# An LSTM recurrence on one core: gate banks by halves, four tanh, and output sums by accumulating transfers

## The chip, the core and the metric

The kernel runs on one core of a Trainium2 chip. A core has TensorE (PE, with its weight loads shown as PEld), VectorE (DVE), ScalarE (ACT), GpSimd (POOL) and SyncE (SP), which only issues transfers; ACT and POOL issue transfers too. The engines run beside each other and wait for each other by semaphores. The metric is the device time of one execution, in microseconds (us), the median of several runs.

## What is computed

Two layers over x of shape (32, 512, 256), fp32: 32 batch rows, 512 places, 256 features. Each layer adds a graph attention block and then a feed-forward block to x. The first three of these four blocks make the first two thirds of the time and are not touched by the change. The fourth block is an LSTM over the 512 places, followed by running sums:

```python
x_proj = jnp.einsum('btd,gd->btg', x, W_ih) + b_ih + b_hh
def step(carry, xp):
    h, c = carry
    gates = xp + h @ W_hh.T
    i, f, g, o = jnp.split(gates, 4, axis=-1)
    c = jax.nn.sigmoid(f) * c + jax.nn.sigmoid(i) * jnp.tanh(g)
    h = jax.nn.sigmoid(o) * jnp.tanh(c)
    return ((h, c), h)
...
logits = jnp.einsum('bth,lh->btl', lstm_out, W_lin) + b_lin
g = jax.lax.stop_gradient(jnp.argmax(logits, axis=-1).astype(lstm_out.dtype))[..., None]
w = g * lstm_out
inc = jnp.cumsum(w, axis=1)
prefix = inc - w
suffix = inc[:, -1:, :] - inc
return 2.0 * lstm_out + prefix * fw_att + suffix * bw_att
```

The x that goes in is a layer norm of the layer's x, and the result is added to x. There are two logits, so that `g` is 0 or 1.

## The kernel before

The first stage (`layers_per_batch`) goes through the 32 batch rows and leaves x in device memory as X3 (places, batch, features). In it, POOL prepares the LSTM's weights piece by piece (`recurrence_weights`, lines 1180 to 1287): it scales the gates, lays them out in the order g, f, i, o (`order`, `half`, `ordered`) and writes them to `wr`.

The second stage is `recurrence` (line 1290 on). The 256 features are four quarters q of 64, and each quarter is two halves of H = 32. All tiles of a step have 128 partitions: 4 quarters x 32 batch rows. Column tiles of PE (32 output partitions each) make the four quarters.

Gates stand in two banks of PSUM (`PARTS`, line 1406): bank 0 has g, f, i of the first halves (96 columns), bank 1 has g, f, i of the second halves, o of both halves, and two columns that carry the logits (162 columns). `part` (line 1408) multiplies one operand into the banks, in an order of pairs (k, n): k is the half of the contraction, n the bank, each with four matmuls, one for each quarter. All matmuls are fp32.

A step t of the loop at line 1444 does this:

1. PE adds the part of `h` to the banks of step t, in the order (0,0), (0,1), (1,0), (1,1) (line 1465); `h[0]` and `h[1]` are the transposed halves of the last step. Then it starts the banks of step t + 1 with the part of x (`x_part`, line 1418).
2. ACT takes tanh of bank 0 (line 1472, 96 columns) and of bank 1 (line 1473, 160 columns). The sigmoids are tanh too, by scaled weights.
3. VectorE makes, for each half, `ab` (line 1478) and the new c in `z2` (line 1481).
4. ACT takes tanh of c for each half (line 1483), and copies one column (line 1485).
5. VectorE makes `hh` (line 1491) and its transpose `h` (line 1495) for each half. These release the next step's matmuls.
6. VectorE makes `g` (line 1502) from the logits in bank 1 and `hh` of the step before, does one filler from the list `extra` (line 1506), and adds to the running sum `pp` (line 1508). At a chunk's first step it also copies `pp` (line 1510).

A chunk is 16 steps (CH), and in each chunk 16 fillers are done, one in each step. Four are statistics of the next chunk's x (`stats`, lines 1335 to 1339; the last one has POOL make `ve` and `rs`, lines 132 and 134), two are norms of two tiles each (`both`, line 1457, with `norm` at line 1341), and ten are the results of the chunk before (`results`, line 1360): in two halves of 8 places, x3 = x3 + hh + pp * fw - pp' * bw, five operations on 512 columns each. The last one is followed by four transfers of x3 to the tile R (line 1399), which holds all outputs. SP loads x (line 1331) and x3 (line 1364). PE turns the normed x in steps 5, 6, 10 and 11 (`turn`, line 1347).

The order of PE, VectorE and ACT is the order of the program's text (line 1425). The order of SP and POOL is made by a scheduler. A buffer that is read by a transfer or another engine is not written before that is done.

After the loop (lines 1511 to 1531), `tot` is the total of the sum times bw (the weights fw and bw are halved at line 1253). 16 transfers spread it over all partitions into `tots`; the last chunk's results follow; and then, in 17 pieces of up to 8 places, VectorE adds `tots` to R and SP and ACT send R to the output.

Of the kernel before, what the change touches and what calls it, by code (L numbers as in the profile page):

```python
# [9 lines left out]
F32 = mybir.dt.float32  # L10
# [9 lines left out]
P = 128  # L20
# [1159 lines left out]
def recurrence_weights(nc, pool, a, wr, now):  # L1180
# [18 lines left out]
    def ordered(raw, n, quarters, s):  # L1199

        t = tile_(P, 2 * W, "rwt")
        tq = t.rearrange("p (q w) -> p q w", q=2)[:n, :quarters]
        rq = raw.rearrange("p (q w) -> p q w", q=quarters)[:n]
        nc.gpsimd.memset(tq[:, :, 4 * J :], 0.0)
        for to, g in enumerate(order):
            src = rq[:, :, g * J : (g + 1) * J]
            if to < 3:
                for e in range(2):
                    nc.gpsimd.tensor_scalar(
                        tq[:, :, (3 * e + to) * 32 : (3 * e + to + 1) * 32], src[:, :, e * 32 : (e + 1) * 32],  # L1210
                        half[g] * s, None, ALU.mult,
                    )
            else:
                nc.gpsimd.tensor_scalar(tq[:, :, 3 * J : 4 * J], src, half[g] * s, None, ALU.mult)
        return t, tq
# [37 lines left out]
    nc.gpsimd.tensor_scalar(t[:, : 2 * J], t[:, : 2 * J], 0.5, None, ALU.mult)  # L1253
# [36 lines left out]
def recurrence(ctx, tc, c, a, X3, wr, out):  # L1290
# [27 lines left out]
    R = wp.tile([P, TQ, D], F32, name="R")  # L1318

# [40 lines left out]
    def results(t0, hh, pp):  # L1360

        x3 = ch.tile([P, CH, J], F32, tag="x3", name=f"x3_{t0}")
        for q in range(Q):
            nc.sync.dma_start(
                out=x3[q * GB : (q + 1) * GB],
                in_=X3[t0 : t0 + CH, :, q * J : (q + 1) * J].rearrange("t b j -> b t j"),
            )
        todo = []
        n = CH // 2
        for s in (slice(0, n), slice(n, CH)):  # L1370
            r = x3[:, s, :]
            pf = pp[:, s.start : s.stop, :]
            pb = pp[:, s.start + 1 : s.stop + 1, :]
            m = st.tile([P, n, J], F32, tag="m", bufs=1, name=f"m{t0}_{s.start}")
            bc = [P, n, J]

            def one_(r=r, s=s):
                nc.vector.tensor_tensor(r, r, hh[:, s, :], ALU.add)  # L1378

            def two_(m=m, pf=pf):  # L1380
                nc.vector.tensor_tensor(m, pf, fw.unsqueeze(1).to_broadcast(bc), ALU.mult)  # L1381

            def three(r=r, m=m):
                nc.vector.tensor_tensor(r, r, m, ALU.add)  # L1384

            def four(m=m, pb=pb):
                nc.vector.tensor_tensor(m, pb, bw.unsqueeze(1).to_broadcast(bc), ALU.mult)  # L1387

            def five(r=r, m=m):
                nc.vector.tensor_tensor(r, r, m, ALU.subtract)  # L1390

            todo += [one_, two_, three, four, five]
        last_ = todo.pop()

        def gathered():
            last_()
            tq, r0 = t0 // TQ, t0 % TQ
            for q in range(Q):
                nc.sync.dma_start(
                    out=R[tq * GB : (tq + 1) * GB, r0 : r0 + CH, q * J : (q + 1) * J], in_=x3[q * GB : (q + 1) * GB]  # L1400
                )

        return todo + [gathered]


    PARTS = ((0, 3 * H), (3 * H, W))

    def part(pg, w, lhs, order, start, stop):

        for k, n in order:  # L1410
            p, (s, e) = pg[n], PARTS[n]
            for q in range(Q):
# [5 lines left out]
    def x_part(t, xT):  # L1418
# [3 lines left out]
        part(pg, wih, [xT[t % CH // G][:, k, r : r + GB] for k in range(DK)], ((0, 0), (1, 0), (0, 1), (1, 1)), True, t == 0)  # L1422
        return pg

    with tc.manual_schedule(engines={mybir.EngineType.PE, mybir.EngineType.DVE, mybir.EngineType.Activation}):
# [18 lines left out]
        for t in range(T + 1):  # L1444
            s = t % CH
            last = t == T
            if s == 0 and not last:
# [9 lines left out]
                both = [lambda fs=norms[n : n + 2]: [f() for f in fs] for n in range(0, len(norms), 2)]  # L1457
                extra = stats + both + more
                turning = {(5, 6, 10, 11)[n]: f for n, f in enumerate(turns)}
            if last:  # L1460

                pg = [None, psg.tile([P, W - 3 * H], F32, tag="pg1", name="pglast")]
                part(pg, whh, h, ((0, 1), (1, 1)), True, True)
            elif t:
                part(pg, whh, h, ((0, 0), (0, 1), (1, 0), (1, 1)), False, True)
            pgs = pg
            if not last:
# [4 lines left out]
                nc.scalar.activation(z[:, H : 4 * H], pgs[0], AF.Tanh)  # L1472
                nc.scalar.activation(z[:, 5 * H : 10 * H], pgs[1][:, : 5 * H], AF.Tanh)
# [23 lines left out]
            if t:  # L1497
# [5 lines left out]
                    g_, pgs[1][:, 5 * H : 5 * H + 1].to_broadcast([P, J]), level, h_[:, i, :], ALU.is_gt, ALU.mult,  # L1503
# [11 lines left out]
        tots = wp.tile([P, D], F32, name="tots")  # L1515
        for n in range(4 * Q):
            tq, q = n // Q, n % Q
            (nc.sync, nc.scalar, nc.gpsimd)[n % 3].dma_start(
                out=tots[tq * GB : (tq + 1) * GB, q * J : (q + 1) * J], in_=tot[q * GB : (q + 1) * GB]
            )  # L1520
        for f in results(T - CH, hh, pp):
            f()
        t0 = 0
        for step in [2, 6] + [8] * (TQ // 8 - 1):
            r = R[:, t0 : t0 + step, :]
            nc.vector.tensor_tensor(r, r, tots.unsqueeze(1).to_broadcast([P, step, D]), ALU.add)  # L1526
# [4 lines left out]
            t0 += step  # L1531

# [123 lines left out]
```

## Time and profile before

| | us |
|---|---|
| median of 3 runs | 3859.15 (3856.74 to 3864.42) |
| the profiled execution | 3853.91 |
| its span | 3852.2 |
| stage 1, from 0 to about 2540 | PE busy 2356.98, DVE 2062.08, ACT 1794.45, POOL 1448.21 |
| recurrence, 2540 to 3787 | PE busy 1060.81, DVE 1152.43, ACT 608.58, POOL 59.84 |
| tail, 3787 to 3853 | DVE busy 41.94, transfers 265 GB/s |

The granted clock of TensorE was 0.98 in stage 1 and 0.99 in the recurrence. Times in the views are microseconds from the start of the span. A row of the timeline has its start, its length, the engine, the line of the kernel, the operation with what it writes and reads, how often it comes in a row, and in brackets the engine's idle time before it with what ended that. A matmul's end is modelled, so starts are the safer numbers. Matmuls of a row that overlap are merged into one length.

### The profile page before, as it was taken

The page shows a single profiled execution, that of the slowest core. Times are in us where ns is not written, and L with a number is a line of the kernel's source. Part 1 is how long each engine was busy: PE and PEld are TensorE (multiplying, and loading weights), DVE is VectorE, ACT ScalarE, POOL GpSimd, SP SyncE. Part 2 cuts the span into 40 slices and gives each one's busy share as a digit, 9 for nine tenths or more (in the row PEclk, how much of TensorE's full clock was granted, in tenths as well). Part 3 has the DMA queues.
Part 4 walks back from the last instruction along what each step waited for, and adds up shares of the span by engine and source line. Part 5 has one row for each costly group of instructions (what it writes and reads, how often), then busy time and mean ns, then how long its engine had stood idle before and what let it go on. Part 6 is the DMA issues. An engine that isn't in the chain of part 4 may idle for free. (4 is left out here: it accounts for less than half of the span.)

```text
span 3852.2 us, 117182 instructions
## 1 busy us (share of the span) xinstructions
PE 3417.8 (89%) x47370; PEld 2313.5 (60%) x47370; DVE 3256.5 (85%) x10671; ACT 2403.0 (62%) x6434; POOL 1510.6 (39%) x1581
## 2 busy tenths in 40 slices
PE   5999999999999999999999998668888888888882
PEld 3466566556656656655665664446666666666661
DVE  3888888888888888888888886459999999999997
ACT  2777777777777777777777775435454544444441
POOL 3456556555555655655555566710000000000000
PEclk8999999999999999999999998789999999999996
DMA  3322322222223232232223212221222222222226
GB/s 98 89 91 73 101 85 75 94 86 86 83 93 90 72 102 86 72 95 86 86 83 96 87 61 59 82 66 41 44 46 43 46 43 46 43 46 43 46 40 191
DMA packets 271800, 288.76 MB, mean 75 GB/s; under 512 B 151589, under 2 KB 221953, under 8 KB 269073
## 3 DMA queue, kind: packets, MB, share of 16 engines
q1 hardware_dynamic: 265248, 266.96, 25.0%
q10 hardware_dynamic: 3152, 8.76, 0.7%
q8 instruction: 375, 6.14, 0.7%
q0 software_dynamic: 2848, 5.45, 0.5%
q14 instruction: 177, 1.44, 0.1%
HBM read 227.09 MB, written 37.11 MB: 69 GB/s over the span
## 5 line engine op out<-in xcount | busy, mean ns | idle before, releaser
L1413 PE MATMUL pg<-wall,h 128*32 128x96 f32 x16352 | 559.0, 277 | 176.8 <-DVE h L1495 169.4
L1413 PEld LDWEIGHTS pg<-wall,h 128*32 128x32 f32 x16352 | 374.4, 109 | 350.8 <-DVE h L1495 331.9
L1413 PE MATMUL pg<-wall,xTr 128*32 128x96 f32 (+1 forms) x16384 | 549.0, 274 | 0.0
L1413 PEld LDWEIGHTS pg<-wall,xTr 128*32 128x32 f32 x16384 | 447.2, 110 | 5.2 <-issue 0.3
L132 POOL TENSOR_SCALAR ve<-mv 128x4 f32<-128x4 f32 x32 | 6.3, 195 | 1038.5 <-DVE mv L1337 1038.5
L1472 ACT ACTIVATE z<-pg 128x96 f32<-128x96 f32 x512 | 128.7, 251 | 438.9 <-PE pg L1413 438.9
L102 DVE SCALAR_TENSOR_TENSOR w<-rb,colsa,adjT 128x512 f32<-128x512 f32 x512 | 380.4, 778 | 6.0 <-DMA rb<-linea 6.0
L102 DVE SCALAR_TENSOR_TENSOR acc<-px,convw,acc 128x511 f32<-128x511 f32 (+2 forms) x480 | 335.3, 735 | 7.6 <-ACT acc L102 6.4
L1483 ACT ACTIVATE z<-z 128x32 f32<-128x32 f32 x1024 | 234.7, 229 | 168.5 <-DVE z L1481 100.9
L102 ACT ACTIVATE g<-bc,cs 128x128 f32<-128x128 f32 x1024 | 326.0, 399 | 13.1 <-PE py L102 13.1
L102 PE MATMUL px<-mT,win 128*128 128x512 f32 x640 | 307.2, 603 | 0.0
L102 PE MATMUL po<-wc,xh 128*128 128x256 f32 x1024 | 254.3, 392 | 13.5 <-POOL xh L102 8.4
L102 POOL TENSOR_SCALAR ve<-bnmv 128x4 f32<-128x4 f32 x96 | 18.8, 196 | 626.3 <-DVE bnmv L102 607.7
L102 PE MATMUL pav<-w,hb 128*64 128x512 f32 x1024 | 250.1, 608 | 8.0 <-DVE w L102 8.0
L102 PE MATMUL pov<-wb,wv 128*128 128x257 f32 x1024 | 250.5, 392 | 7.0 <-DVE wv L102 5.8
L1495 DVE STREAM_TRANSPOSE h<-hh 128x32 f32<-128x32 f32 x1024 | 216.4, 211 | 34.8
L102 PE MATMUL pz<-mT,win 128*128 128x512 f32 x512 | 245.4, 602 | 0.0
L102 POOL TENSOR_TENSOR rs<-ve,mhalf 128x4 f32<-128x4 f32 (+1 forms) x192 | 237.8, 1239 | 13.3
L1478 DVE SCALAR_TENSOR_TENSOR ab<-z 128x64 f32<-128x64 f32 x1024 | 226.0, 221 | 15.3 <-ACT z L1472 12.0
L102 PEld LDWEIGHTS po<-wc,xh 128*128 128x128 f32 x1024 | 189.5, 193 | 76.6 <-issue 27.0
L1481 DVE SCALAR_TENSOR_TENSOR z<-ab 128x32 f32<-128x32 f32 x1024 | 196.9, 192 | 35.1
L102 POOL TENSOR_SCALAR msk<-adj 128x1024 bf16<-128x1024 int32 x64 | 218.8, 3434 | 13.0 <-DMA adj<-in_adj_dram 7.9
(258 smaller groups left out, 7987.8 us busy)
## 6 DMA issues: line engine op xcount, KB each, us to landing
bc<-line SPq DMA_DIRECT2D x128, 512.0 KB
adj<-in_adj_dram SPq DMA_DIRECT2D x32, 1024.0 KB
rb<-linea SPq DMA_DIRECT2D x64, 512.0 KB
ce<-line SPq DMA_DIRECT2D x64, 384.0 KB
x<-in_x_dram SPq DMA_DIRECT2D x32, 512.0 KB
X<-x SPq DMA_DIRECT2D x32, 512.0 KB
xt<-X SPq DMA_DIRECT2D x128, 128.0 KB
x<-X SPq DMA_DIRECT2D x128, 128.0 KB
```

Of the source, the lines that this page charges most:

```text
L102: return getattr(getattr(self.nc, engine), op)(*map(real, a), **{n: real(v) for n, v in k.items()})
L132: nc.gpsimd.tensor_scalar(ve, var, scale, eps, ALU.mult, ALU.add)
L1413: nc.tensor.matmul(p[q * GB : (q + 1) * GB, :], lhs[k], w[:, k, q, s:e], start=(start and k == 0), stop=(stop and k == DK - 1),)
L1472: nc.scalar.activation(z[:, H : 4 * H], pgs[0], AF.Tanh)
L1478: nc.vector.scalar_tensor_tensor(ab, z[:, c0 + 2 * H : c0 + 4 * H], 1.0, z[:, c0 : c0 + 2 * H], ALU.add, ALU.mult)
L1481: nc.vector.scalar_tensor_tensor(z2[:, c0 : c0 + H], ab[:, :H], 0.5, ab[:, H:], ALU.mult, ALU.add)
L1483: nc.scalar.activation(z[:, (10 + n) * H : (11 + n) * H], z2[:, 4 * n * H : (4 * n + 1) * H], AF.Tanh, scale=0.5)
L1495: nc.vector.transpose(h[n], half)
```

## The change

- The gates are laid out as g, f, i, o of the first halves, then g, f, i, o of the second halves and the logits' columns. So bank 0 has 128 columns and bank 1 has 130.
- ACT has four tanh in place of two: of 96 and of 32 columns in bank 0, then of 96 and of 32 in bank 1.
- The matmuls of `h` come in the order (0,0) for all quarters, (0,1) for quarters 0 and 1, (1,0) for all, (0,1) for quarters 2 and 3, (1,1) for all.
- The results are sums by transfers of POOL that accumulate into x3: `hh` as it is, pp * fw, and pp' * bw with the sign of bw turned (line 1253 becomes a multiply by 0.5 and one by -0.5). VectorE only makes the products, in eight fillers of 256 columns; norms are one tile to a filler, and PE turns x in steps 6, 7, 10 and 11. A chunk still has 16 fillers.
- After the loop, `tots` is made by four matmuls with `sel`, a tile of ones and zeros that POOL copies from the identity before the loop. The outputs subtract it. The last chunk's results are done between the first outputs.

```diff
         nc.gpsimd.memset(tq[:, :, 4 * J :], 0.0)
         for to, g in enumerate(order):
             src = rq[:, :, g * J : (g + 1) * J]
-            if to < 3:
-                for e in range(2):
-                    nc.gpsimd.tensor_scalar(
-                        tq[:, :, (3 * e + to) * 32 : (3 * e + to + 1) * 32], src[:, :, e * 32 : (e + 1) * 32],
-                        half[g] * s, None, ALU.mult,
-                    )
-            else:
-                nc.gpsimd.tensor_scalar(tq[:, :, 3 * J : 4 * J], src, half[g] * s, None, ALU.mult)
+            for e in range(2):
+                nc.gpsimd.tensor_scalar(
+                    tq[:, :, (4 * e + to) * 32 : (4 * e + to + 1) * 32], src[:, :, e * 32 : (e + 1) * 32],
+                    half[g] * s, None, ALU.mult,
+                )
         return t, tq
     def begun(t, *columns):
...
         for q in range(Q):
             nc.gpsimd.dma_start(out=t[q * GB : (q + 1) * GB, n * J : (n + 1) * J], in_=src[q : q + 1, :].to_broadcast([GB, J]))
         yield
-    nc.gpsimd.tensor_scalar(t[:, : 2 * J], t[:, : 2 * J], 0.5, None, ALU.mult)
+    for n, scale in enumerate((0.5, -0.5)):
+        nc.gpsimd.tensor_scalar(t[:, n * J : (n + 1) * J], t[:, n * J : (n + 1) * J], scale, None, ALU.mult)
     yield
     nc.gpsimd.dma_start(out=wr[:, n0 : n0 + 2 * J], in_=t[:, : 2 * J])
     yield
...
     TQ = T // 4
     R = wp.tile([P, TQ, D], F32, name="R")
+    sel = wp.tile([P, Q, P], F32, name="sel")
+    for q in range(Q):
+        nc.gpsimd.tensor_copy(
+            sel[:, q, :].rearrange("p (t b) -> p t b", b=GB),
+            c.ident[:, q * GB : (q + 1) * GB].unsqueeze(1).to_broadcast([P, 4, GB]),
+        )
     NX = CH // 4
...
                 out=x3[q * GB : (q + 1) * GB],
                 in_=X3[t0 : t0 + CH, :, q * J : (q + 1) * J].rearrange("t b j -> b t j"),
             )
+        nc.gpsimd.dma_start(out=x3, in_=hh, accum_op=ALU.add)
         todo = []
-        n = CH // 2
-        for s in (slice(0, n), slice(n, CH)):
-            r = x3[:, s, :]
-            pf = pp[:, s.start : s.stop, :]
-            pb = pp[:, s.start + 1 : s.stop + 1, :]
-            m = st.tile([P, n, J], F32, tag="m", bufs=1, name=f"m{t0}_{s.start}")
-            bc = [P, n, J]
-
-            def one_(r=r, s=s):
-                nc.vector.tensor_tensor(r, r, hh[:, s, :], ALU.add)
-
-            def two_(m=m, pf=pf):
-                nc.vector.tensor_tensor(m, pf, fw.unsqueeze(1).to_broadcast(bc), ALU.mult)
-
-            def three(r=r, m=m):
-                nc.vector.tensor_tensor(r, r, m, ALU.add)
-
-            def four(m=m, pb=pb):
-                nc.vector.tensor_tensor(m, pb, bw.unsqueeze(1).to_broadcast(bc), ALU.mult)
-
-            def five(r=r, m=m):
-                nc.vector.tensor_tensor(r, r, m, ALU.subtract)
-
-            todo += [one_, two_, three, four, five]
+        for n, w in enumerate((fw, bw)):
+            m = ch.tile([P, CH, J], F32, tag=f"m{n}", bufs=1, name=f"m{n}_{t0}")
+            for s in range(0, CH, 4):
+
+                def product(n=n, w=w, m=m, s=s):
+                    nc.vector.tensor_tensor(
+                        m[:, s : s + 4, :], pp[:, s + n : s + n + 4, :], w.unsqueeze(1).to_broadcast([P, 4, J]), ALU.mult
+                    )
+                    if s + 4 == CH:
+                        nc.gpsimd.dma_start(out=x3, in_=m, accum_op=ALU.add)
+
+                todo.append(product)
         last_ = todo.pop()
         def gathered():
...
         return todo + [gathered]
-    PARTS = ((0, 3 * H), (3 * H, W))
+    PARTS = ((0, 4 * H), (4 * H, W))
+    ALL = tuple(range(Q))
+    WHOLE = tuple((k, n, ALL) for n in range(2) for k in range(DK))
+    LATER = ((0, 0, ALL), (0, 1, ALL[:2]), (1, 0, ALL), (0, 1, ALL[2:]), (1, 1, ALL))
     def part(pg, w, lhs, order, start, stop):
-        for k, n in order:
+        for k, n, qs in order:
             p, (s, e) = pg[n], PARTS[n]
-            for q in range(Q):
+            for q in qs:
                 nc.tensor.matmul(
                     p[q * GB : (q + 1) * GB, :], lhs[k], w[:, k, q, s:e],
                     start=(start and k == 0), stop=(stop and k == DK - 1),
...
         pg = [psg.tile([P, e - s], F32, tag=f"pg{n}", name=f"pg{n}_{t}") for n, (s, e) in enumerate(PARTS)]
         r = (t % G) * GB
-        part(pg, wih, [xT[t % CH // G][:, k, r : r + GB] for k in range(DK)], ((0, 0), (1, 0), (0, 1), (1, 1)), True, t == 0)
+        part(pg, wih, [xT[t % CH // G][:, k, r : r + GB] for k in range(DK)], WHOLE, True, t == 0)
         return pg
     with tc.manual_schedule(engines={mybir.EngineType.PE, mybir.EngineType.DVE, mybir.EngineType.Activation}):
...
                 xT, nxt = nxt, [None] * 2
                 stats, norms, turns = normalised(t0 + CH, nxt) if t0 + CH < T else ([], [], [])
                 more = results(t0 - CH, hh_was, pp_was) if t else []
-                both = [lambda fs=norms[n : n + 2]: [f() for f in fs] for n in range(0, len(norms), 2)]
-                extra = stats + both + more
-                turning = {(5, 6, 10, 11)[n]: f for n, f in enumerate(turns)}
+                extra = stats + more[:1] + norms + more[1:] if t else stats + norms
+                turning = {(6, 7, 10, 11)[n]: f for n, f in enumerate(turns)}
             if last:
-                pg = [None, psg.tile([P, W - 3 * H], F32, tag="pg1", name="pglast")]
-                part(pg, whh, h, ((0, 1), (1, 1)), True, True)
+                pg = [None, psg.tile([P, W - 4 * H], F32, tag="pg1", name="pglast")]
+                part(pg, whh, h, WHOLE[DK:], True, True)
             elif t:
-                part(pg, whh, h, ((0, 0), (0, 1), (1, 0), (1, 1)), False, True)
+                part(pg, whh, h, LATER, False, True)
             pgs = pg
             if not last:
                 if t + 1 < T:
                     pg = x_part(t + 1, xT if t + 1 < t0 + CH else nxt)
                 turned = [turning.pop(s)()] if s in turning else []
-                nc.scalar.activation(z[:, H : 4 * H], pgs[0], AF.Tanh)
-                nc.scalar.activation(z[:, 5 * H : 10 * H], pgs[1][:, : 5 * H], AF.Tanh)
+                for n in range(2):
+                    nc.scalar.activation(z[:, (4 * n + 1) * H : (4 * n + 4) * H], pgs[n][:, : 3 * H], AF.Tanh)
+                    nc.scalar.activation(z[:, (8 + n) * H : (9 + n) * H], pgs[n][:, 3 * H : 4 * H], AF.Tanh)
                 z2 = st.tile([P, 12 * H + 1], F32, tag="z", name=f"z{t + 1}")
                 for n in range(2):
                     c0 = 4 * n * H
...
                 p_, h_ = (pp_was, hh_was) if s == 0 and not last else (pp, hh)
                 g_ = st.tile([P, J], F32, tag="g", name=f"g{t}")
                 nc.vector.scalar_tensor_tensor(
-                    g_, pgs[1][:, 5 * H : 5 * H + 1].to_broadcast([P, J]), level, h_[:, i, :], ALU.is_gt, ALU.mult,
+                    g_, pgs[1][:, 4 * H : 4 * H + 1].to_broadcast([P, J]), level, h_[:, i, :], ALU.is_gt, ALU.mult,
                 )
             if extra and not last:
                 extra.pop(0)()
...
         tot = wp.tile([P, J], F32, name="tot")
         nc.vector.tensor_tensor(tot, pp[:, CH, :], bw, ALU.mult)
-        tots = wp.tile([P, D], F32, name="tots")
-        for n in range(4 * Q):
-            tq, q = n // Q, n % Q
-            (nc.sync, nc.scalar, nc.gpsimd)[n % 3].dma_start(
-                out=tots[tq * GB : (tq + 1) * GB, q * J : (q + 1) * J], in_=tot[q * GB : (q + 1) * GB]
-            )
-        for f in results(T - CH, hh, pp):
-            f()
+        tots = psx.tile([P, DK, P], F32, tag="px", name="tots").rearrange("p k e -> p (k e)")
+        for q in range(Q):
+            nc.tensor.matmul(
+                tots[:, q * J : (q + 1) * J],
+                sel[:, q, :], tot,
+                start=True, stop=True,
+            )
+        rest = results(T - CH, hh, pp)
         t0 = 0
-        for step in [2, 6] + [8] * (TQ // 8 - 1):
+        for n, step in enumerate([2, 6] + [8] * (TQ // 8 - 1)):
+            assert not rest or t0 + step <= TQ - CH
             r = R[:, t0 : t0 + step, :]
-            nc.vector.tensor_tensor(r, r, tots.unsqueeze(1).to_broadcast([P, step, D]), ALU.add)
+            nc.vector.tensor_tensor(r, r, tots.unsqueeze(1).to_broadcast([P, step, D]), ALU.subtract)
             for tq in range(4):
                 (nc.sync, nc.scalar)[tq % 2].dma_start(
                     out=out[:, tq * TQ + t0 : tq * TQ + t0 + step, :], in_=r[tq * GB : (tq + 1) * GB]
                 )
             t0 += step
+            if n:
+                for f in rest[:4]:
+                    f()
+                rest = rest[4:]
```

## The prediction, made before the changed kernel ran

> **What bounds the kernel now.** I read the page first, then the timeline of single steps of the recurrence, the chain of waits in the same stretch, and last the stages of the tail. The page's chain of waits puts VectorE in front:
>
> ```profile
> DVE 27%; PE 3%; issue 2%; DMA 1%; ACT 1%; SPq 0%; DVEq 0%
> ```
>
> That line misleads here. The recurrence is a loop of 512 steps, and most of them carry one filler operation on VectorE (lines 1336 to 1390). Two steps, the first with a filler of 512 columns, the second with none, both from the timeline (start, length in us, engine, line, operation):
>
> ```profile
> 3200.26 0.25 ACT L1472 ACTIVATE z<-pg 128x96 f32<-128x96 f32 x1 [0.96 <-PE pg L1413]
> ...
> 3202.17 0.68 DVE L1384 TENSOR_TENSOR x<-x,m 128x512 f32<-128x512 f32 x1
> ...
> 3202.66 0.25 ACT L1472 ACTIVATE z<-pg 128x96 f32<-128x96 f32 x1 [0.96 <-PE pg L1413]
> ```
>
> ```profile
> 2583.62 0.25 ACT L1472 ACTIVATE z<-pg 128x96 f32<-128x96 f32 x1 [0.96 <-PE pg L1413]
> ...
> 2585.14 0.77 PEld L1413 LDWEIGHTS pg<-wall,h 128*32 128x32 f32 x32 [0.75 <-DVE h L1495]
> 2585.14 1.09 PE L1413 MATMUL pg<-wall,h 128*32 128x96 f32 x32 [0.43 <-DVE h L1495]
> 2585.24 0.21 DVE L1495 STREAM_TRANSPOSE h<-hh 128x32 f32<-128x32 f32 x1
> ...
> 2586.02 0.25 ACT L1472 ACTIVATE z<-pg 128x96 f32<-128x96 f32 x1 [0.96 <-PE pg L1413]
> 2586.30 0.30 ACT L1473 ACTIVATE z<-pg 128x160 f32<-128x160 f32 x1
> 2586.30 0.23 DVE L1478 SCALAR_TENSOR_TENSOR ab<-z 128x64 f32<-128x64 f32 x1 [0.43 <-ACT z L1472]
> 2586.57 0.19 DVE L1481 SCALAR_TENSOR_TENSOR z<-ab 128x32 f32<-128x32 f32 x1
> 2586.67 0.22 DVE L1478 SCALAR_TENSOR_TENSOR ab<-z 128x64 f32<-128x64 f32 x1
> 2586.79 0.59 ACT L1483 ACTIVATE z<-z 128x32 f32<-128x32 f32 x2 [0.19 <-DVE z L1481]
> 2586.92 0.19 DVE L1481 SCALAR_TENSOR_TENSOR z<-ab 128x32 f32<-128x32 f32 x1
> 2587.05 0.19 DVE L1491 SCALAR_TENSOR_TENSOR hh<-z 128x32 f32<-128x32 f32 x1
> ```
>
> From first tanh to first tanh, the step with a filler takes 2.40 us (3200.26 to 3202.66), and so does the step without (2583.62 to 2586.02), where VectorE idles 0.43 us before `ab`. So fillers are covered. The bound is the ring transpose `h`, matmuls, tanh, `ab`, `z`, tanh of c, `hh`, transpose. The source view of line 1472 runs from 2550.8 to 3783.8: 1233.0 us for 511 intervals, 2.413 each. The excess over 2.40 is 6.6 us, mostly one step in 16 of 2.51 us, at a chunk's start (2593.22 to 2595.73), where line 1510 adds a copy.
>
> **The ring in numbers.** In the weight loads of the same step (a narrower window), the second half's first load stands at 2585.50, 0.36 after the first half's and 0.26 after its transpose began at 2585.24: it waits for `h1`. The first tanh follows 0.52 later, as soon as bank 0 has its last matmuls. Four matmuls on the four column tiles start as a quartet:
>
> ```profile
> 2585.14 0.29 PE L1413 MATMUL pg<-wall,h 128*32 128x96 f32 x4 [0.43 <-DVE h L1495]
> ```
> ```profile
> 2585.14 0.37 PE L1413 MATMUL pg<-wall,h 128*32 128x96 f32 x8 [0.43 <-DVE h L1495]
> ```
>
> Eight end only 0.08 us after four, so a quartet of 96 columns costs 0.08. Each fp32 matmul of the program is two records, hence each group of four is two quartets. The x part's 32 loads take 0.88 us for 4 quartets of 96 columns and 4 of 162, 1032 columns: 0.85 ns a column. A quartet of 128 to 130 columns is then 0.11 (an estimate).
>
> **Banks and order of matmuls (lines 1406 to 1422).** Bank 0 grows from 96 to 128 columns (o of the first half joins it); bank 1 shrinks from 162 to 130.
> 1. Ahead of `h1`: two quartets of bank 0 (0.22) and the piece of bank 1 on tiles 0 and 1. If a half quartet lasts as long as a full one, 0.22 more: 0.44. The second half's matmuls can start at 0.36 + 0.11 for the load = 0.47. So `h1` still decides; the piece brings nothing there.
> 2. First tanh: bank 0's last two quartets are 32 columns wider each, 2 x 32 x 0.85 ns = 0.055. It comes 0.575 after the load, not 0.52, though it reads the same 96 columns: it waits for the bank's last matmul.
> 3. Second tanh: today two quartets of 162 later, 2 x 0.138 = 0.276 (trace: 2586.30 less 2586.02 = 0.28). Afterwards the rest of the split piece (two quartets) and then the second half's part (two) come in between: 4 x 0.11 = 0.44.
> 4. VectorE: the second `ab` stands 0.65 after the first tanh, set by the first `ab` and `z`. With tanh at 0.44 and 0.28 from tanh to `ab`, it stands at 0.72. On to `z` 0.25, tanh of c 0.22, `hh` 0.26, transpose 0.23, load 0.26 (all differences of starts above or in the step before), first tanh 0.575: 0.72 + 0.25 + 0.22 + 0.26 + 0.23 + 0.26 + 0.575 = **2.51 us a step**. The same sum with 0.65 and 0.52 gives 2.39, against 2.40 seen. 511 x 0.11 = **+56 us**.
>
> No row shows two tiles alone. Bounds: at worst as above; at best a half piece costs half, the second tanh comes at 0.33, `ab` stays at 0.65, and the step is 2.40 + 0.055 = 2.455, +28 us. I take the worst, because four matmuls already run abreast and none is seen to go faster for fewer neighbours. [...]
>
> **Four tanh (lines 1472, 1473).** ACT gets two more instructions of 32 columns. Today's 32-column tanh takes 0.23, and the copy behind it starts 0.14 after it (2584.75 to 2584.89). ACT has the first tanh at 0 and the third at 0.44, and tanh of c waits for `z` until 0.77 (2586.79 less 2586.02); 0.14 fits behind each. Nothing; without that cover 0.14 a step.
>
> **Fillers and transfers (lines 1360 to 1403).** Per chunk ten operations of 0.68 become eight of 256 columns (about 0.35), norms go one to a step: VectorE saves about 4 us a chunk, all of it idle time, since the step without filler is no shorter. Only the chunk's first step has no cover: with a longer ring its 0.11 excess shrinks by about 0.04, 31 x 0.04 = **-1.5 us**. The accumulating transfers, three of 512 KB a chunk, are issued by POOL and run one behind another. POOL's transfers of 258 KB land in 2.4 us (DMA view), so one takes 2.4 to 5. In the built order POOL holds the sum of `hh`, then that of `m1`, then the chunk's `ve` and `rs` (lines 132, 134), which VectorE's first norm needs in step 5. `m1` is ready in step 15; five steps are 12 us. SP's copies to R wait for the last sum, with the next x loads behind them, which are due a chunk later. Hidden, unless a sum takes over 10 us.
>
> POOL beside VectorE: while `rs` ran (2601.05, 1.01), one `z` took 0.22 for 0.19 and the step 2.43. Three issues a chunk at 0.02 make 2 us, within the rounding. [...]
>
> **Tail.** Today `tot` (3786.76) goes out in 16 transfers, VectorE then does the last chunk's ten fillers, and the outputs leave from 3794.55 on. From 3800 the transfers are full:
>
> ```profile
> 3794.00:3800.00 6.00, 0.00 (x0) 0.00 (x0) 6.00 (x4) 0.00 (x0) 0.00 (x0) 0.50 0.79 176
> 3800.00:3810.00 10.00, 0.00 (x0) 0.00 (x0) 10.00 (x6) 0.00 (x0) 0.00 (x0) 0.50 0.97 316
> 3810.00:3820.00 10.00, 0.00 (x0) 0.00 (x0) 10.00 (x5) 0.00 (x0) 0.00 (x0) 0.50 1.01 338
> ```
>
> (the last two columns: busy share of the DMA engines, GB/s). With four matmuls instead, outputs start near 3789, 5.5 us earlier, but three sums of the last chunk add 1.5 MB, 4.7 us at 338 GB/s if counted once, twice that if a sum reads both sides. SP also stands before its copy of the last chunk until all three have landed, while ACT's queue goes on. -6 to +8; I take **-2**. The copies that make `sel` (POOL) stand in its 17.73 us idle before line 132: nothing; uncovered, under 1.3. One more multiply per weight piece on POOL lies in the first stage, where POOL is no bound.
>
> **Sum.** 3853.9 (the profiled execution; its span is 3852.2) + 56 - 1.5 - 2 = **3906**. The median of the runs, 3859.15, lies 5 above that execution, inside the range.
>
> **Rivals.**
> - Only the wider bank costs (half pieces at half price): 3853.9 + 28 - 1.5 - 2 = 3878. For it: no row of two tiles. Against: the quartets.
> - POOL's sums are late: `rs` behind them holds the norm and so the ring, in each chunk. At 1 us a chunk, 32 more: 3938. For it: POOL serves them in order. Against: 12 us of room for 2.4 to 5.
> - Faster: the ring stays at 2.40, because PE's idle wait for `h1` takes in the wider quartets (records of bank 0 abreast with those of the load). Then tail and chunk starts remain, -6 and -3: 3845. It decides if the first tanh starts at most 0.52 after the second half's first load and the third at most 0.37 after it. Against: today's first tanh comes only after the last quartet.
> - The order isn't as written: the built order of PE, ACT and VectorE is; POOL and SP are free, which is the second rival.
>
> **Chances.** Forecast 0.62, wider bank alone 0.14, late sums 0.15, faster 0.06, no change by cancelling 0.03. The range must reach to 3868 (wider bank with a tail of -8 or so) and to 3942 (late sums). 0.2% is 7.7 us, about what can be told from no change here: faster 0.06, same 0.03, slower 0.91.
>
> **What would show it.** In the changed kernel: steps of 2.51 with and without fillers alike; first tanh 0.575 after the second half's first load; third tanh 0.44 after the first; second `ab` waiting for it. A third tanh at 0.33 means half pieces are cheap; ACT busy when `z` is ready means that four tanh cost; VectorE waiting for POOL in step 5 means late sums. I am wrong if `h1` comes earlier than 0.36 after `h0`.

## The result: 3895.59 us, 0.96% slower

The changed kernel takes 3895.59 us (median of 4 runs, 3894.42 to 3898.47), the kernel before on the same chip 3857.94 (4 runs). The ratio is 1.0096, 95% interval 1.0081 to 1.0111. Forecast were 3906 us and a range of 3868 to 3942. The direction and the range held; the step that made the 3906 did not, as the traces show. The profiled executions are 3853.91 us before (span 3852.2) and 3894.42 after (span 3892.7), both at a granted clock of 0.975.

**Where the 40.5 us of span are.** The first tanh of each step (line 1468 after, 1472 before) cuts the span in three: up to the first step 2557.3 us (before 2550.8), the 511 intervals of the loop 1264.1 (1233.0), from the last first tanh to the end 71.4 (68.4): +6.5, +31.1, +3.0. The median step went from 2.400 to 2.455.

The page's chain of waits of the changed kernel now puts PE ahead of VectorE, where before it was VectorE 27%, PE 3%:

```profile
PE 17%; DVE 12%; ACT 3%; issue 2%; DMA 1%; SPq 0%; DVEq 0%; POOL 0%; ACTq 0%
```

The same turn shows in the page's groups of instructions, `ab` before and after (count, then busy us and mean ns, then idle time of VectorE just ahead and its releaser):

```profile
L1478 DVE SCALAR_TENSOR_TENSOR ab<-z 128x64 f32<-128x64 f32 x1024 | 226.0, 221 | 15.3 <-ACT z L1472 12.0
```
```profile
L1474 DVE SCALAR_TENSOR_TENSOR ab<-z 128x64 f32<-128x64 f32 x1024 | 227.0, 222 | 130.3 <-ACT z L1468 123.1
```

The operation costs the same; VectorE now waits 115 us more in front of it. That is more than the loop lost, because the smaller fillers (0.42 us of 256 columns for 0.68 of 512) left VectorE more idle time as well. One step from the timeline of the changed kernel:

```profile
3372.71 1.12 PE L1409 MATMUL pg<-wall,h 128*32 128x128 f32 x30 [0.35 <-DVE h L1491]
...
3373.64 0.25 ACT L1468 ACTIVATE z<-pg 128x96 f32<-128x96 f32 x1 [1.02 <-PE pg L1409]
...
3373.79 0.19 ACT L1469 ACTIVATE z<-pg 128x32 f32<-128x32 f32 x1
3373.93 0.23 DVE L1474 SCALAR_TENSOR_TENSOR ab<-z 128x64 f32<-128x64 f32 x1 [0.28 <-ACT z L1468]
3373.99 0.25 ACT L1468 ACTIVATE z<-pg 128x96 f32<-128x96 f32 x1
...
3374.18 0.19 DVE L1477 SCALAR_TENSOR_TENSOR z<-ab 128x32 f32<-128x32 f32 x1
3374.30 0.22 DVE L1474 SCALAR_TENSOR_TENSOR ab<-z 128x64 f32<-128x64 f32 x1
3374.41 0.59 ACT L1479 ACTIVATE z<-z 128x32 f32<-128x32 f32 x2
...
3376.10 0.25 ACT L1468 ACTIVATE z<-pg 128x96 f32<-128x96 f32 x1 [0.50 <-PE pg L1409]
```

Four readings. The first tanh comes 0.93 after the step's first matmul (0.88 before: 2585.14 to 2586.02). The third tanh, that of the second half, comes 0.35 after the first, not 0.44. So the second `ab` has no bracket: it follows `z` without idle time, 0.65 after the first tanh, as before. And first tanh to first tanh is 2.46: the step grew by the 0.055 of the wider first bank and by nothing else.

**The tail** in the view by windows (columns as in the prediction; the last two are the busy share of the DMA engines and GB/s):

```profile
3832.00:3838.00 6.00, 0.00 (x0) 0.00 (x0) 6.00 (x7) 0.00 (x0) 0.86 (x1) 0.50 1.01 233
3838.00:3848.00 10.00, 0.00 (x0) 0.00 (x0) 10.00 (x6) 0.00 (x0) 0.00 (x0) 0.50 0.95 252
3848.00:3858.00 10.00, 0.00 (x0) 0.00 (x0) 10.00 (x6) 0.00 (x0) 0.00 (x0) 0.50 1.00 285
3858.00:3868.00 10.00, 0.00 (x0) 0.00 (x0) 6.59 (x3) 0.00 (x0) 0.00 (x0) 0.50 1.00 346
```

The first output leaves 5.95 after the last first tanh (3821.35 to 3827.30), where it left 10.80 after it before: 4.9 us won. But for 26 us the DMA engines are full at 233 to 285 GB/s. In the kernel before, the full stretches ran at 316 GB/s and more, up to this one:

```profile
3830.00:3840.00 10.00, 0.00 (x0) 0.00 (x0) 0.00 (x0) 0.00 (x0) 0.00 (x0) 0.50 1.00 342
```

Against 342 that is 2.1 MB short, 6 us at that rate. In the tail the accumulating transfers stand in a DMA queue of their own: its 1.57 MB are three of 512 KB. Its row, from the last first tanh to the end (3821.35 to 3892.70; packets, MB, share of the 16 engines):

```profile
q0 software_dynamic: 432, 1.57, 12.6%
```

12.6% of 71.3 us are 9.0 us of all 16 engines for the three sums, about twice the 4.6 us that 1.57 MB take at 342 GB/s.

### The profile page after: what moved, and what is told of

The parts are those of the page before. It is cut to its first block, busy times and chain, and to the rows that moved or that the text cites. A ratio compares the mean times of both kernels' runs of the same rounds, so it can differ in the third digit from the quotient of the medians.

```text
span 3892.7 us, 118956 instructions
## 1 busy us (share of the span) xinstructions
PE 3493.8 (90%) x47378; PEld 2436.7 (63%) x47378; DVE 3169.5 (81%) x10607; ACT 2463.8 (63%) x7458; POOL 1588.7 (41%) x1690
## 5 line engine op out<-in xcount | busy, mean ns | idle before, releaser
L1409 PE MATMUL pg<-wall,h 128*32 128x128 f32 x16352 | 631.7, 278 | 134.4 <-DVE h L1491 131.9
L1409 PEld LDWEIGHTS pg<-wall,h 128*32 128x32 f32 x16352 | 491.9, 109 | 266.0 <-DVE h L1491 262.3
L1409 PE MATMUL pg<-wall,xTr 128*32 128x128 f32 (+1 forms) x16384 | 621.9, 274 | 3.8 <-issue 3.8
L1468 ACT ACTIVATE z<-pg 128x96 f32<-128x96 f32 x1024 | 256.3, 250 | 466.6 <-PE pg L1409 462.6
L1409 PEld LDWEIGHTS pg<-wall,xTr 128*32 128x32 f32 x16384 | 535.9, 110 | 5.8 <-issue 5.3
L102 PEld LDWEIGHTS pov<-wb,wv 128*128 128x128 f32 x1024 | 186.3, 192 | 59.7 <-issue 24.4
```

The source lines that it names most:

```text
L102: return getattr(getattr(self.nc, engine), op)(*map(real, a), **{n: real(v) for n, v in k.items()})
L1409: nc.tensor.matmul(p[q * GB : (q + 1) * GB, :], lhs[k], w[:, k, q, s:e], start=(start and k == 0), stop=(stop and k == DK - 1),)
L1468: nc.scalar.activation(z[:, (4 * n + 1) * H : (4 * n + 4) * H], pgs[n][:, : 3 * H], AF.Tanh)
```

## The experiments

The theory: the loop pays for the wider first bank, since the first tanh waits for the bank's last matmuls, and a little for stalls that come with the accumulating transfers; the split piece, the four tanh and the fillers cost nothing. The main rival: the transfers cost most. A second question is what holds the second half's matmuls, their load (the prediction's reading) or the matmuls queued ahead of them.

**1. Only the ring.** Banks, weights' order, four tanh and split piece of the change; sums, fillers and tail as before. This is the changed kernel's `PARTS`, `LATER` and tanh in the kernel before:

```diff
-    PARTS = ((0, 3 * H), (3 * H, W))
+    PARTS = ((0, 4 * H), (4 * H, W))
...
+    LATER = ((0, 0, ALL), (0, 1, ALL[:2]), (1, 0, ALL), (0, 1, ALL[2:]), (1, 1, ALL))
```

> Banks of f, i, g, o, four tanh and the split piece as in the changed kernel; the outputs' sums on VectorE, the fillers and the tail as before. Theory (the wider first bank is the cost): the step is 2.455 us, as in the changed kernel, first tanh 0.58 after the second half's first load, third tanh 0.34 after the first; loop +28 us against before, start +0 to +6, tail 0: ratio 1.007 to 1.009. Rival (the accumulating transfers cost most of the 37 us): the loop is 10 us longer or less, ratio under 1.004.

Measured: 3880.72 against 3851.78 us, ratio 1.0076 (1.0062 to 1.0090). Step 2.455, third tanh 0.346 after the first, second `ab` at 0.654. The loop is 1257.3, +24.3: 511 intervals of 0.055 are 28, less 1.8 that the steps at the chunks' starts (2.507, was 2.509) no longer add, 1.1 at the loop's very first step (2.94, was 3.98) and 0.6 in one filler step of each chunk. The ring is three quarters of the loss.

**2. Only the sums.** The other half of the change, on the banks of before: `results`, the order of `extra` and `turning`, and the tail.

```diff
+        nc.gpsimd.dma_start(out=x3, in_=hh, accum_op=ALU.add)
...
+                    if s + 4 == CH:
+                        nc.gpsimd.dma_start(out=x3, in_=m, accum_op=ALU.add)
```

> Accumulating transfers, fillers, turns and tail as in the changed kernel; banks, tanh and order of matmuls as before. Theory: steps stay at 2.40, some steps of a chunk stall, together about 5 us over the loop; tail +3: ratio 1.001 to 1.003. Rival (the transfers cost most): loop +20 us or more, ratio over 1.005.

Measured: 3861.89, ratio 1.0024 (1.0015 to 1.0033). Loop 1237.1 (+4.1), tail 72.8 (+4.4). The two halves, 28.9 and 10.1 us by the medians, add to 39.0; the whole change cost 37.7. The main rival falls.

The loop's 4 us are some eleven long steps (over 0.15 above the median), up to 3.37 us. One of them in the timeline, and the DMA engines around it (from 3190 to 3220, 30 us in 40 slices, busy tenths):

```profile
3217.98 0.64 PE L1409 MATMUL pg<-wall,h 128*32 128x162 f32 x16 [0.64 <-issue]
```
```profile
DMA  0889200000240074999400000000999999910003
```

The PE's bracket names no engine: `h` had been there since 3217.0, and the PE waited for "issue", which is how the profile calls idle time that no engine or transfer in it explains. The full slices at 3211 to 3216 are two accumulating transfers, one behind the other (288 packets, the last few of them later). The trace also has a queue "instruction" with packets of 16 KB (below called blocks), which took 1.4% of the same 16 DMA engines' time before: 250 packets in the 1190 us from 2580 to 3770, one for two steps of 128 loads and matmuls. The views count 255 loads and matmuls for each packet there, and 255 in experiments 7 and 9 too, with 192 and 144 a step. That a block holds some 255 of PE's instructions is an estimate from these counts. Ahead of the stall these blocks start at 3208.59 and 3215.75, 7.2 apart, for a median of 4.7. Blocks more than 6 us apart: 2 before, 1 with the ring alone, 31 here, 25 in the changed kernel. In each of these last 56 gaps lie 50 to 288 packets of accumulating transfers; of the other gaps, about one in five has that many.

The records also tie the pauses themselves to the blocks. The block that starts at 3215.75 has landed at 3216.70, and PE goes on 1.28 later, at 3217.98. In eight of the eleven long steps PE or its weight loads pause with no engine named and go on 1.2 to 1.5 us after a block has landed; these eight are 4.4 us longer than the median step, together. In the changed kernel it is all eight of its long steps behind the loop's first, 5.6 us together.

**3. The sums twice.** Each accumulating transfer is issued a second time into a tile that nothing reads (with a memset of it).

```diff
...
+                        nc.gpsimd.dma_start(out=twice, in_=m, accum_op=ALU.add)
```

> The kernel with accumulating transfers and new tail on the banks of before, with each accumulating transfer issued a second time into a tile that nothing reads (one more memset a chunk on POOL). Theory (the stalls of the loop are PE waiting for its instructions while these transfers fill the DMA engines): PE's idle time for issue in the loop rises from 2.6 us to 5 to 15, the loop gets longer by the same, and the tail by some 4 to 8. Rival (the stalls come from the fillers' new order or from VectorE waiting for data): issue time stays under 3 us, the loop within 2 us of the single sums.

Measured: 3926.01, ratio 1.0180 (1.0166 to 1.0194); loop 1284.3, tail 85.3. The size was missed: the loop grew by 51 us over before, not by 5 to 15. But it grew where the theory says. What PE waited for in the loop, from the view of waits (total us, times, longest): the changed kernel, this one, and the one with three banks below.

```profile
PE pg L1409 <- issue: 5.4, 6, 1.4
```
```profile
PE pg L1413 <- issue: 36.5, 42, 2.0
```
```profile
PE pg L1413 <- issue: 197.9, 265, 2.2
```

The kernel before has no such line, and with the single sums it was 1.9 us, 4 times. All 42 pauses of the second row end 1.2 to 1.6 us after a block has landed. The 46 steps of the loop with such a pause hold 45 of the 58 us by which the loop exceeds 2.40 a step. The added memset is a rival that the trace can settle: it takes 0.95 a chunk, and VectorE's operations beside it are as long as without it (`ab` 0.22, `z` 0.19). So here transfers for which no step of the loop was seen to wait still cost time, in pauses of PE that end after a block has landed, and the price rose faster than the traffic (the loop's 51 us for 4, with 91.8 MB for 48.2 in the 1190 us from 2580).

**4. The new tail alone**, with VectorE's sums: totals by matmuls, two of the last chunk's ten operations after each output.

```diff
-        for f in results(T - CH, hh, pp):
-            f()
...
+        rest = results(T - CH, hh, pp)
...
+            if n:
+                for f in rest[:2]:
+                    f()
+                rest = rest[2:]
```

> The kernel before with one part of the change: the totals by four matmuls and the last chunk's sums between the outputs, these sums still on VectorE; loop and transfers as before. Theory (the accumulating transfers, 1.5 MB beside the outputs, are what makes the tail longer): first output some 5 us earlier, tail 63 against 68, ratio 0.998 to 0.9995. Rival (the new order of the tail itself costs, as VectorE's sums then stand between the outputs): tail 68 to 73, ratio 1.000 to 1.001.

Measured: 3852.77, ratio 0.9992 (0.9983 to 1.0001), tail 65.3. The tail is 3 us shorter without the accumulating transfers and 4 longer with them (72.8 above): they cost some 7.5 us there and turn its gain into a loss. By the medians alone the gain is not told from none.

**5. The piece whole, ahead.** In the changed kernel:

```diff
-    LATER = ((0, 0, ALL), (0, 1, ALL[:2]), (1, 0, ALL), (0, 1, ALL[2:]), (1, 1, ALL))
+    LATER = ((0, 0, ALL), (0, 1, ALL), (1, 0, ALL), (1, 1, ALL))
```

> The changed kernel, but the first half's part for the second bank is in one piece, ahead of the second half's matmuls. Theory (the queue of matmuls ahead of the second half's, some 0.44 us, sets its start, and VectorE's first ab and z set the second ab): first tanh still 0.58 after the second half's first load, third tanh about 0.23 after the first, second ab 0.65 after it; step 2.455, the same time as the changed kernel within 3 us. Rival (the split piece costs): the step falls to 2.43 or less, 10 us or more below the changed kernel. Rival (the split helps): the step rises by 0.03 or more, 15 us above it.

Measured: 3887.67, ratio 1.0093 (1.0077 to 1.0108), not told from the changed kernel's. Step 2.455, third tanh at 0.225, second `ab` at 0.652. Two quartets of 130 take 0.225; the split puts 0.12 on top, one quartet's worth, not two. In the records of single matmuls one sees why (they give the widths; which tile it is follows from the program's order): in the changed kernel's step from 3372.71, tiles 0 and 1 start the piece at 3372.95 and the second half's matmuls at 3373.17; tiles 2 and 3, which have no piece yet, start these at 3373.08 and are at the piece from 3373.32 on. The pairs of tiles run apart by about 0.1, so half pieces overlap. It neither helps nor harms, because VectorE reaches the second `ab` at 0.65 either way.

**6. Nothing ahead of the second half.**

```diff
+    LATER = ((0, 0, ALL), (1, 0, ALL), (0, 1, ALL), (1, 1, ALL))
```

> The changed kernel, but nothing of the second bank stands ahead of the second half's matmuls for the first bank: the first half's part for the second bank follows them whole. Theory (the load takes some 0.03, the queue of 0.44 held the second half's matmuls): they start at 0.39 after the first half's first load, the first tanh comes 0.50 after the second half's first load (0.58 in the changed kernel); the second bank then needs four quartets of 0.11 after it, so the third tanh comes 0.43 after the first and the second ab waits for it, at 0.71; step 2.44 to 2.45, within 8 us of the changed kernel. Rival (the prediction's price, a load of 0.11): first tanh 0.58, third tanh 0.44, second ab 0.72, step 2.51, 28 us above the changed kernel.

Measured: 3892.22, ratio 1.0093 (1.0077 to 1.0108). From its timeline:

```profile
3301.81 0.25 ACT L1468 ACTIVATE z<-pg 128x96 f32<-128x96 f32 x1 [0.94 <-PE pg L1409]
...
3302.25 0.25 ACT L1468 ACTIVATE z<-pg 128x96 f32<-128x96 f32 x1
...
3302.53 0.23 DVE L1474 SCALAR_TENSOR_TENSOR ab<-z 128x64 f32<-128x64 f32 x1
```

First tanh 0.494 after the second half's first load (0.573 in the changed kernel), third tanh 0.443 later, second `ab` at 0.725: step 2.459. So 0.08 is won at the first tanh and lost at the second `ab`. The load of 0.11 falls: with it, 0.58 would have stayed. And four quartets in a row do take 0.44, the price the prediction had for the changed order; only there two of them overlap.

**7. Three banks**, on the kernel before: 96 columns of each half in a bank of their own, o of both halves and the logits in a third, last in the order.

```diff
-    PARTS = ((0, 3 * H), (3 * H, W))
+    PARTS = ((0, 3 * H), (3 * H, 6 * H), (6 * H, W))
...
-                part(pg, whh, h, ((0, 0), (0, 1), (1, 0), (1, 1)), False, True)
+                part(pg, whh, h, ((0, 0), (0, 1), (1, 0), (1, 1), (0, 2), (1, 2)), False, True)
```

> The kernel before with o of both halves and the logits in a third bank, whose matmuls stand last: first bank 96 columns, second 96, third 66; tanh of first half, of second half, of both o. Theory (the second half's matmuls are held by the 0.44 us of matmuls queued ahead, not by their load): ahead of them stand four quartets of 96 columns, 0.33; they start at 0.39 to 0.40, the first tanh comes 0.45 after the second half's first load (0.52 before), the step is 2.33: 36 us less than before, about 3820. Rival (the prediction's reading, that a load takes 0.11 and holds them until 0.47): first tanh stays at 0.52 and the step at 2.40, no change within 6 us; if 16 more matmuls in each of the two parts delay PE, slower.

Measured: 4059.91, ratio 1.0544 (1.0529 to 1.0558): neither reading saw this; only the last clause, with no number, has the sign. Two steps of its timeline:

```profile
2577.43 0.25 ACT L1472 ACTIVATE z<-pg 128x96 f32<-128x96 f32 x1 [1.70 <-PE pg L1413]
...
2579.75 0.25 ACT L1472 ACTIVATE z<-pg 128x96 f32<-128x96 f32 x1 [0.32 <-PE pg L1413]
```

Where nothing disturbs it, the step is 2.32, as the theory of the queue had it. But the median is 2.806. With 96 loads and 96 matmuls a step, and 255 of them to a block by the estimate of experiment 2, PE needs three quarters of a block each step, a block in 1.33 steps. The queue of the blocks between 2580 and 3770 (packets, MB, share of the engines), in the kernel before and in this one:

```profile
q8 instruction: 250, 4.10, 1.4%
```
```profile
q8 instruction: 319, 5.23, 1.8%
```

The blocks start 3.68 us apart here (median), though one takes only 1.02: 0.75 x 3.68 = 2.76 us a step. That alone would only say that blocks and steps keep pace; what shows which of them waits is the third line of waits above, 265 pauses of PE for "issue", 198 us. Each of them ends 1.2 to 1.6 us after a block has landed (median 1.4), and the next block starts 1.2 after PE has gone on (median). 1.2 + 1.0 + 1.4 are 3.6 us a block, and the 255 instructions would take 255/192 x 2.32 = 3.1 us in undisturbed steps. The kernel before, with 128 loads and matmuls in 2.40 us, shows no wait of PE for "issue" in the loop; this one, with 192, shows 198 us.

**8. o between.** To save instructions: two banks as before, and only the first half's part for the second bank cut by columns, 72 pairs a step instead of 64.

```diff
-                part(pg, whh, h, ((0, 0), (0, 1), (1, 0), (1, 1)), False, True)
+                part(pg, whh, h, ((0, 0), (0, 1, 0, 3 * H), (1, 0), (0, 1, 3 * H, W - 3 * H), (1, 1)), False, True)
```

> The kernel before with the first half's part for the second bank cut by columns: f, i, g (96) ahead of the second half's matmuls for the first bank, o and the logits (66) behind them; 72 matmul pairs a step for 64. Theory: ahead stand four quartets of 96, 0.33, and the second half's matmuls start with their load at 0.39, 0.07 earlier; second tanh at 0.39 after the first, second ab at 0.67: step 2.33 to 2.35, 25 to 36 us less than before. Rival (PE cannot take its instructions faster: in the kernel with three banks PE stood idle some 200 us for issue alone): issue waits of 10 us or more, step above 2.40, no gain.

Measured: 3857.56, ratio 1.0004 (0.9995 to 1.0013); 0.2 us of issue, step 2.407. First tanh 0.441 after the second half's first load, as expected. The miss is in the second: it comes at 0.39, but reads 160 columns, and `ab` follows 0.34 later instead of 0.28, at 0.73 for 0.65. What the first tanh won, the second `ab` lost.

**9. o last**, with a tanh of its own for both o.

```diff
-                part(pg, whh, h, ((0, 0), (0, 1), (1, 0), (1, 1)), False, True)
+                part(pg, whh, h, ((0, 0), (0, 1, 0, 3 * H), (1, 0), (1, 1), (0, 1, 3 * H, W - 3 * H)), False, True)
...
-                nc.scalar.activation(z[:, 5 * H : 10 * H], pgs[1][:, : 5 * H], AF.Tanh)
+                nc.scalar.activation(z[:, 5 * H : 8 * H], pgs[1][:, : 3 * H], AF.Tanh)
+                nc.scalar.activation(z[:, 8 * H : 10 * H], pgs[1][:, 3 * H : 5 * H], AF.Tanh)
```

> The kernel before with the first half's part for the second bank cut by columns: f, i, g (96) ahead of the second half's matmuls for the first bank, o and the logits (66) last of all; a tanh of its own for the two o (three a step for two); 72 matmul pairs a step for 64. Theory: the second half's matmuls start with their load (0.39 after the first half's), the first tanh comes 0.44 after that load (0.52 before), the second tanh 0.28 after the first, the second ab at 0.65: step 2.32 to 2.34, 30 to 40 us less than before, ratio 0.990 to 0.992. Rival (the tanh of f, i, g of the second half waits for the whole bank, its o columns too): second tanh at 0.39, second ab at 0.67, step 2.34 to 2.36. Rival (instruction supply): PE idle for issue 20 us or more, no gain.

Measured: 3834.03, ratio 0.9940 (0.9927 to 0.9954), faster than both kernels. From its timeline:

```profile
3255.80 0.25 ACT L1475 ACTIVATE z<-pg 128x96 f32<-128x96 f32 x1 [0.88 <-PE pg L1416]
...
3256.12 0.22 DVE L1482 SCALAR_TENSOR_TENSOR ab<-z 128x64 f32<-128x64 f32 x1
3256.19 0.25 ACT L1476 ACTIVATE z<-pg 128x96 f32<-128x96 f32 x1
...
3256.49 0.22 DVE L1482 SCALAR_TENSOR_TENSOR ab<-z 128x64 f32<-128x64 f32 x1
```

The first rival was right: the second tanh reads 96 finished columns, yet comes at 0.39, after the o columns of its bank. In experiment 7, where these 96 have a bank of their own, it comes at 0.165 (median). Whether the chip or the program's own semaphores make it wait is not shown. Step 2.358; the gain is 18.2 us in the loop (1214.8) and not the 36 that 2.33 would give. Most of the rest is this wait: in steps without a wide filler the second `ab` stands at 0.67 and the step is 2.35. The fillers add a little. Under those of 512 columns the first `ab` comes at 0.32, not 0.28, with no idle time ahead of it, in this kernel and in experiment 8 (there at a step of 2.407): the first tanh comes earlier behind `h`, and VectorE has less time for a filler in between. The two steps with two norms each and the chunks' first steps stay at 2.40 and 2.51.

**10. o last with the new tail** (edits 9 and 4 together).

> The kernel just described with the changed kernel's new tail as well (totals by matmuls, the last chunk's sums between the outputs, by VectorE, no accumulating transfers). Theory: gains add, 3 us below the kernel without the tail: ratio 0.988 to 0.991. Rival: the tail's gain is not seen beside it (within 2 us).

Measured: 3835.59, ratio 0.9942 (0.9928 to 0.9955). The profiled tail is shorter (65.1 for 68.3), the medians show no difference; the rival holds as far as the runs can tell.

## Why the prediction was right, and where it was not

- **Direction and range held**; the likeliest value was 10 us too high. The step that failed is the third point of the ring's working: "4 x 0.11 = 0.44" for the second tanh. It measured 0.345, the best bound given there (0.33), since half quartets on two pairs of tiles overlap: the records under experiment 5 have tiles 0 and 1 at the piece from 3372.95 to 3373.17, and tiles 2 and 3 at the second half's matmuls from 3373.08 on. With it falls "I take the worst": the rival "only the wider bank costs", put at 3878, is what the ring did (2.455, experiments 1 and 5).
- **First tanh 0.575 after the load**: 0.573 (median). The estimate of 0.85 ns a column held: 2 x 32 columns cost 0.055, and four quartets 0.443.
- **"h1 still decides"** failed. The load takes 0.024 (last section); the second half's matmuls stood behind 0.44 of matmuls in both kernels (0.33 without them gave a first tanh 0.44 after the load, experiments 8 and 9). The sum came out right, as 0.47 is also where the queue ends.
- **Four tanh: nothing; fillers: nothing; POOL's issues: nothing; chunk start**: as forecast, though a filler of 256 columns takes 0.42, not 0.35, and the issue of a sum 0.92, where those of `tots` before took 0.50. VectorE's operations beside an issue are as long as without one (`ab` 0.22, `z` 0.19). Chunk starts stayed at 2.51 while other steps grew, worth 1.7 for the forecast 1.5.
- **Accumulating transfers "hidden"**: not quite. They land in 5.1 (`hh`) and 6.3 us (products; both medians in the loop), above the estimated 2.4 to 5. No `rs` was late, so the rival of late sums fell by its mechanism; what came late beside them were the blocks (25 gaps over 6 us in the changed kernel, 2 before), on no list of the prediction: about 4 us in the loop of experiment 2, 5.4 us of issue in the changed kernel's profiled execution. The size varies: the kernels of experiments 5 and 6 have the same transfers and 0.7 and 1.4 us of issue.
- **Tail -2**: +3.0, with the sign turned. The earlier start (5.5 forecast, 4.9 seen) and the sums' traffic were both named. The term that was mis-sized is the traffic: 4.7 if counted once, twice that if a sum reads both sides, and it measured 9.0 us of all engines, 7.5 by experiment 4. The -2 was below even the sum with one count (-5.5 + 4.7 = -0.8); with two it gives +3.9.
- **First stage**: forecast at nothing, seen +6.5 in the profiled execution. Its start of the loop varies from 2548.5 to 2554.7 over eight kernels with the weights' code of before or one multiply more, and from 2550.2 to 2557.3 over the four with the changed code. Whether the extra multiplies cost a few us there stays open.

So the 3895 is 28 for the bank less 1.7 and smaller savings, some 5 of stalls, 3 of tail, and up to 6.5 ahead of the loop; the 3906 had 56 for the ring, -1.5 and -2, and nothing for stalls or start. That it came so near is partly luck: the ring was priced 28 us too high, and about half of that was made up by stalls, tail and start, which the sum had at nothing or below.

## What to carry to other kernels

Price a piece of work on some column tiles by each tile's own queue (the split piece put 0.12 ahead of the third tanh, where two quartets in a row would have put 0.22), and ask what stands queued ahead of an instruction before crediting its wait to its data (here 0.44 of matmuls, for a load of 0.024). In these kernels a tanh waited for the last matmul into its bank, wanted columns or not (the second at 0.39 with o in its bank, experiment 9; at 0.165 without, experiment 7): the bank's width was the price. Count instructions and bulk transfers for a small-matmul loop: PE was idle for "issue" for 198 us with 192 loads and matmuls a step (experiment 7), and for 36.5 us beside the doubled accumulating transfers (experiment 3).

## What the runs showed of the hardware that was not expected

- The 16 KB packets of the queue "instruction" start 3.68 us apart (median) in experiment 7, though one takes 1.02; PE goes on some 1.4 us after one has landed, and the next starts some 1.2 us after that. 128 loads and matmuls in 2.40 us ran without a wait of PE for "issue" (the kernel before), 144 in 2.36 with 1.2 us of it in the loop (experiment 9, on the x part), 192 with 198 us.
- Beside two accumulating transfers of 512 KB in a row (3211.2 to 3216.3, experiment 2) the next block starts 7.2 us after the one before it, for a median of 4.7. No run here shows where the 2.5 us arise.
- A weight load ahead of a matmul on a 128 x 32 tile costs 0.024: in the changed kernel's step from 3372.71 the records that open with their load are 0.297 long, those whose load ran ahead 0.273.
